# Query product of token tile 0 ahead of the first scores, x by ScalarE's queue and W by SyncE's

## The chip, the core and the metric

The kernel runs on one core of a Trainium2 chip. A core has TensorE (PE, matrix products; its weight loads are listed apart as PEld), VectorE (DVE), ScalarE (ACT), GpSimd (POOL) and SyncE (SP), each with its own instruction queue, worked off in order, and 16 DMA engines that all queues share. Times are device microseconds (us) of one execution. The metric is that time; the kernel before takes 636.64 us (median of three runs, 636.23 to 636.75).

## The reference

Three layers over 8 x 64 = 512 tokens of width 512, all in 32-bit floats. The change concerns the first one, a cross attention over a context of 1601 rows for each of the 8 sequences:

```python
def _L0_xattn_ref(proj_p, proj_q, W, b):     # proj_p = layernorm(x), proj_q = context
    trans_q = jnp.einsum('bqh,oh->bqo', proj_q, W) + b
    att_weights = jnp.einsum('bph,bqh->bpq', proj_p, trans_q)
    att_norm = jax.nn.softmax(att_weights, axis=-1)
    att_vec = jnp.einsum('bpq,bqh->bph', att_norm, proj_q)
    return jax.nn.relu(jnp.einsum('bph,oh->bpo', att_vec, W) + b)
x = x + _L0_xattn_ref(_layernorm(x), ctx_1024, W, b)
```

After it come a causal linear attention with a GELU network (2048 wide), and a mixture of 8 experts of which each token takes two. They fill the time from about 170 us to the end and are not changed.

## The kernel before, in words

The 512 tokens are four tiles of 128 tokens (t = 0 to 3); a tile holds two sequences (h = 0, 1) of 64 tokens. The kernel does not multiply the 1601 context rows by W. It multiplies the normalised tokens by W once ("query product", `pw_t`, 128 x 4 x 512) and takes scores between that and the transposed context.

The front, before the first scores:

- x comes in two halves (line 101), tiles 0 and 1 by SP's queue and tiles 2 and 3 by ACT's; then W by SP (line 113); then SP issues the stream of context tiles.
- 12 idle matmuls on PE (line 224) run while x is under way.
- `statistics` (lines 353 to 360: mean and variance on DVE, square root on ACT) and `normalize` (362 to 366, DVE) for tiles 0 and 1, then for 2 and 3. Their outputs `pn` live in the buffer `xin`.
- `turn_p(t)` (370 to 374): four transposes of a normalised tile on PE into a PSUM bank, copied by ACT into `p_t`, which lives in `h_t`.
- W is transposed whole, 16 transposes into four PSUM banks (line 405), which DVE copies to `w_t` (line 411). `w_t` is used for the output of the layer, from 70 us on.
- `pw_half(half, hc)` (379 to 390): the query product of two token tiles (256 columns) for one of four blocks of W; four products add up in a bank, and ACT copies the bank to `pw_t`. All four blocks of the first half come before the first scores; the four blocks of the second half stand one each behind the four score groups of tile 0 (line 607).

The attention loop. `key_group(t, g)` (441 to 464): the scores of tile t against a quarter g of the keys (401 or 398 columns), two sequences side by side in the array; ACT copies them out with a bias `pb`, which DVE computes from the normalised tiles and the vector b (417 to 423). After the fourth quarter `softmax(t)` runs: maximum on DVE (469), exponential on ACT (471). `turn_scores(t)` transposes the result on PE (485), `weigh(t, g)` (502 to 535) multiplies it by a group of 512 context rows; the last group adds the tail rows, and the very last context row, which DVE spreads with a shuffle (509). `turn_av` and `attended` (547) apply W, `add_and_normalize` and `turn_h` prepare the next layer's input, `values(t, n)` (575 to 587) computes its value product from `h_t` and the weights `wv`.

The order of the work on each engine is that of the program's text. Only SP's loads run ahead. `stream` (126) writes them into a list, `issue_to` (184) issues them in that order as far as places allow. Context tiles, `wv`'s second half and later weights share a ring of 12 places of 8 KB a partition; a place is free when its reader is `done`. DMAs of all queues take eight semaphores in turn, so SP issues a load when the one eight before it has landed. The list begins with the keys (0, 0), then b (`xb`), keys (0, 1) to (0, 3), the four last rows (`("last", t)`, 8 KB each, placed in parts of `v_sb`), the columns `col` (32 KB), then keys (1, 0) and (1, 1), and for each t in turn rows (t, 0), keys (t+1, 2), rows (t, 1), keys (t+1, 3), rows (t, 2), the tail, and keys (t+2, 0) and (t+2, 1).

Of the kernel before, what the change touches and what calls it, by code (L numbers as in the profile page):

```python
# [20 lines left out]
P = 128  # L21
# [27 lines left out]
def perceiver_kernel(  # L49
# [34 lines left out]
    def mm_bank(name):  # L84
        return ps.tile([P, 512], F32, tag="mm", name=name)
# [11 lines left out]


    xs = resid.tile([P, NT, D], F32, name="xs")
    for t, queue in ((0, nc.sync), (2, nc.scalar)):  # L100
        queue.dma_start(xs[:, t : t + 2, :], x[:, t : t + 2, :])
    moe = ctx.enter_context(tc.tile_pool(name="moe", bufs=1))
    mid = ctx.enter_context(ExitStack())
    xinp = mid.enter_context(tc.tile_pool(name="xinp", bufs=1))
# [21 lines left out]
    def stream(key, src):  # L126
        order.append((key, src))

    def stream_keys(t, g):
        if t < NT:  # L130
            for h in range(2):
                src = context_t[2 * t + h, D * SW * g : D * (SW * g + WIDTHS[g])]
                stream(("ctxT", t, g, h), src.rearrange("(p c k) -> p c k", p=P, c=KC))
# [7 lines left out]
    stream("xb", xb.partition_broadcast(4))  # L141
    for g in range(1, 4):
        stream_keys(0, g)
    for t in range(NT):
        stream(("last", t), context_last[t])
    stream("col", columns)
    for g in range(2):
        stream_keys(1, g)
    for t in range(NT):
        stream_rows(t, 0)  # L150
        stream_keys(t + 1, 2)
        stream_rows(t, 1)
        stream_keys(t + 1, 3)
        stream_rows(t, 2)
        stream(("tail", t), context_tail[t])
        for g in range(2):
            stream_keys(t + 2, g)
        if t == 0:
            stream(("wv", 0), wv[0])
        if t == NT - 2:  # L160
            stream(("wv", 1), wv[1])
# [214 lines left out]

    pw_t = xa.tile([P, KC, B * S], F32, name="pw_t")

    def pw_half(half, hc):
        cols = slice(half * 2 * P, (half + 1) * 2 * P)  # L380
        bank = mm_bank(f"pw_{half}_{hc}")
        for oc in range(KC):
            nc.tensor.matmul(
                bank[:, : 2 * P],
                w_sb[:, oc, hc * P : (hc + 1) * P],
                p_t[:, oc, cols],
                start=(oc == 0),
                stop=(oc == KC - 1),
            )
        nc.scalar.copy(pw_t[:, hc, cols], bank[:, : 2 * P])  # L390

    issue_to(len(order))

    for t in range(0, NT, 2):
        of = [statistics(xs[:, t + h, :], f"p_{t + h}") for h in range(2)]
        for h in range(2):
            normalize(pn[:, t + h, :], xs[:, t + h, :], *of[h], f"p_{t + h}")
        if t == 0:
            turn_p(0)
            turn_p(1)  # L400

            w_banks = [acc_bank(f"w_t_{hc}") for hc in range(KC)]
            for hc in range(KC):
                for oc in range(KC):
                    nc.tensor.transpose(
                        w_banks[hc][:, oc * P : (oc + 1) * P], w_sb[:, oc, hc * P : (hc + 1) * P], ident
                    )
    pw_half(0, 0)
    pw_half(0, 1)
    for hc in range(KC):  # L410
        nc.vector.tensor_copy(w_t[:, hc, :], w_banks[hc])
    turn_p(2)
    turn_p(3)
    pw_half(0, 2)
    pw_half(0, 3)

    nc.vector.stream_shuffle(xb_bc, xb_in, [0] * 32)
    pb = xa.tile([P, NT], F32, name="pb")
# [83 lines left out]
    def weigh(t, g):  # L502

        if g == 0:
            all_av[t] = acc_bank(f"av_{t}")
        av, e_t = all_av[t], all_et[t]
        if g == NG - 1:
            last_bc = xa2.tile([P, D], F32, tag="tmp", name=f"last_bc_{t}")
            nc.vector.stream_shuffle(last_bc, last_in[t], [0] * 32)
        rows = [need("ctx", t, g, h) for h in range(2)]  # L510
        for j in range(4):
            for h in range(2):
                nc.tensor.matmul(  # L513
                    av[h * S : (h + 1) * S, :],
                    e_t[:, 4 * g + j, h * S : (h + 1) * S],
                    rows[h][:, j, :],
                    start=(g == 0 and j == 0),
                    stop=False,
                )
        done(*[("ctx", t, g, h) for h in range(2)])  # L520
        if g == NG - 1:
            for h in range(2):
                nc.tensor.matmul(
                    av[h * S : (h + 1) * S, :],
                    e_t[h * S : (h + 1) * S, 4 * NG, :S],
                    need("tail", t)[h * S : (h + 1) * S, :],
                    start=False,
                    stop=True,
                )
            av_sb = all_av[t] = xa2.tile([P, D], F32, tag="tmp", name=f"av_sb_{t}")  # L530

            nc.vector.scalar_tensor_tensor(
                av_sb, last_bc, all_scores[t][:, LK - 1 : LK], av, ALU.mult, ALU.add
            )
            nc.vector.tensor_scalar(av_sb, av_sb, all_rinv[t], None, ALU.mult)
# [66 lines left out]
            ALU.add,  # L602
        )

    for g in range(4):
        key_group(0, g)
        pw_half(1, g)
    for g in range(2):
        key_group(1, g)
    for t in range(NT):  # L610
# [10 lines left out]
        weigh(t, 1)  # L621
        if t == NT - 1:
            turn_h(t - 1)
        key_group(t + 1, 3)
        if 0 < t < NT - 1:
            values(t - 1, 0)
        weigh(t, 2)
        if t == NT - 2:
            late_loads()
# [1129 lines left out]
```

## Time and profile before

| what | value |
|---|---|
| median of three runs | 636.64 us (636.23 to 636.75) |
| profiled execution | 636.05 us, span 634.3 us |
| PE busy | 617.5 us, 97% of the span |
| DVE, ACT, POOL busy | 182.8, 120.0, 64.1 us |
| mean granted clock of PE | 0.994 |
| DMA | 131.74 MB, mean 208 GB/s, 406 to 428 GB/s from 10 to 160 us |
| first transposes of x on PE | 8.42 us from the span's start |
| first scores of tile 0 | 20.66 us |
| first scores of tile 1 | 39.74 us |

A line of the time line reads: start, duration (both us), engine, line of the kernel, operation, output<-inputs, shape, count; in brackets the idle time before it and what ended that. Equal neighbours are merged, and a duration runs from the first start to the last end. A 32-bit product is two rows (passes) in the trace, a transpose one. A line of the table of stretches gives the stretch, its length, each engine's busy time with its number of instructions, the granted clock of PE (1.00 is full), the DMA engines' busy share and the GB/s moved. A line of the list of waits reads: who waited <- for whom: us in total, times, longest. A queue row reads: queue, packets, MB, share of the DMA engines' time; queue q1 is SP's, q10 ACT's, q0 POOL's.

### The profile page before, as it was taken

What the parts mean: (1) busy time and instruction counts of PE and PEld (TensorE: products, weight loads), DVE (VectorE), ACT (ScalarE), POOL (GpSimd) and SP (SyncE); (2) the same over time, 40 slices, a digit from 0 to 9 for tenths busy, and PEclk for the clock granted to TensorE, in tenths of its full rate; (3) what the DMA queues carried; (4) which work ended last, traced back from release to release, by engine and by line L of the source; (5) the groups of instructions that cost most, each with busy time, mean ns of one, the idle gap of its engine ahead of it and who ended that gap; (6) DMA issues with size and microseconds to landing.
All of it is one profiled execution on the core that took longest, in us unless ns stands there. A gap on an engine that the chain in (4) does not pass through costs nothing. (4 is left out here: it accounts for less than half of the span.)

```text
span 634.3 us, 8728 instructions
## 1 busy us (share of the span) xinstructions
PE 617.5 (97%) x3572; PEld 352.2 (56%) x3572; DVE 182.8 (29%) x433; ACT 120.0 (19%) x225; POOL 64.1 (10%) x87
## 2 busy tenths in 40 slices
PE   7999999999999999999999999999999999999994
PEld 7653434343444444455444447966783667775793
DVE  5111322333326888670000026501311101011100
ACT  2241332320132122031111111301101101111110
POOL 4000000000000000050000002241210121301100
PEclk8999999999999999999999999999999999999998
DMA  8999999999421203030312121426890477784711
GB/s 352 409 422 425 423 422 423 425 428 421 199 67 57 77 2 134 0 132 1 122 35 109 67 100 67 168 79 240 300 367 3 165 295 272 298 327 143 296 19 17
DMA packets 23617, 131.74 MB, mean 208 GB/s; under 512 B 4068, under 2 KB 4068, under 8 KB 12168
## 3 DMA queue, kind: packets, MB, share of 16 engines
q1 hardware_dynamic: 19064, 121.80, 48.5%
q0 software_dynamic: 3248, 7.58, 4.8%
q10 hardware_dynamic: 1248, 1.59, 0.8%
q8 instruction: 38, 0.62, 0.4%
q14 instruction: 19, 0.16, 0.1%
HBM read 126.05 MB, written 4.91 MB: 206 GB/s over the span
## 5 line engine op out<-in xcount | busy, mean ns | idle before, releaser
L1261 PEld LDWEIGHTS up<-xgT,e_up 128*128 128x128 f32 x896 | 100.7, 192 | 4.5 <-ACT y_sb L1239 2.5
L1261 PE MATMUL up<-xgT,e_up 128*128 128x128 f32 x896 | 101.6, 275 | 1.0 <-PEq L1589 0.6
L1227 DVE TENSOR_TENSOR mid<-up,act 128x256 f32<-128x256 f32 x38 | 16.1, 425 | 149.2 <-ACT act L1225 149.2
L1275 PE MATMUL y<-e_wo,mid 128*128 128x512 f32 (+1 forms) x144 | 58.8, 547 | 0.0
L858 PE MATMUL hid<-v_sb,w 128*128 128x512 f32 (+2 forms) x144 | 56.6, 545 | 0.0
L879 PE MATMUL mlp<-w,hid_sb 128*128 128x512 f32 x112 | 51.0, 597 | 0.0
L452 PE MATMUL sc<-ctxT,pw_t 128*64 128x401 f32 (+1 forms) x256 | 46.1, 503 | 0.0
L513 PE MATMUL av<-ctx,eT 128*64 128x512 f32 x192 | 43.5, 597 | 0.0
L858 PEld LDWEIGHTS hid<-v_sb,w 128*128 128x128 f32 x144 | 26.2, 190 | 29.1 <-issue 27.3
L1225 ACT ACTIVATE act<-up 128x256 f32<-128x256 f32 x38 | 14.6, 384 | 120.5 <-PE up L1261 96.7
L1275 PEld LDWEIGHTS y<-e_wo,mid 128*128 128x128 f32 x144 | 25.7, 190 | 20.5 <-issue 17.8
L1240 POOL DMA_INDIRECT out_dram<-y_sb,dst_late x12 | 18.3, 1528 | 166.8 <-ACT y_sb L1239 96.8
L879 PEld LDWEIGHTS mlp<-w,hid_sb 128*128 128x128 f32 x112 | 20.7, 190 | 23.5 <-issue 23.4
L873 POOL TENSOR_TENSOR xin<-xin,b_bc 128x512 f32<-128x512 f32 x4 | 5.1, 1268 | 268.4 <-DVE rstd_h L815 265.0
L452 PEld LDWEIGHTS sc<-ctxT,pw_t 128*64 128x64 f32 x256 | 17.5, 136 | 26.0 <-issue 25.8
L666 PE MATMUL wk<-h_t,wk 128*128 128x512 f32 x64 | 29.5, 604 | 0.0
L666 PE MATMUL wq<-h_t,wq 128*128 128x512 f32 x64 | 29.4, 602 | 0.0
L583 PE MATMUL v<-wv,h_t 128*128 128x512 f32 x64 | 29.2, 599 | 0.0
L777 PE MATMUL wo<-wo,a_t 128*128 128x512 f32 x64 | 28.9, 599 | 0.0
L927 DVE TENSOR_TENSOR xs<-mlp,xs 128x512 f32<-128x512 f32 x3 | 2.1, 691 | 86.5 <-PE mlp L879 86.5
L751 DVE RECIPROCAL rden<-rden 128x512 f32<-128x512 f32 x8 | 26.8, 3353 | 0.3
L513 PEld LDWEIGHTS av<-ctx,eT 128*64 128x64 f32 x192 | 13.0, 136 | 24.2 <-issue 23.9
(263 smaller groups left out, 627.8 us busy)
## 6 DMA issues: line engine op xcount, KB each, us to landing
e_up<-in_L_ffn_up_dram SPq DMA_DIRECT2D x32, 1024.0 KB, 5.3
ctx<-in_ctx_dram SPq DMA_DIRECT2D x24, 1024.0 KB, 17.3
ctxT<-in_ctx_T_dram SPq DMA_DIRECT2D x24, 802.0 KB, 13.3
e_wo<-in_L_ffn_wo_dram SPq DMA_DIRECT2D x16, 1024.0 KB, 10.3
w<-in_L_attn_w_dram SPq DMA_DIRECT2D x8, 1024.0 KB, 6.9
ctxT<-in_ctx_T_dram SPq DMA_DIRECT2D x8, 796.0 KB, 16.2
wv<-in_L_attn_wv_dram SPq DMA_DIRECT2D x2, 1024.0 KB
wq<-in_L_attn_wq_dram SPq DMA_DIRECT2D x2, 1024.0 KB, 17.8
```

The source lines that it names most:

```text
L452: nc.tensor.matmul(sc[h * S : (h + 1) * S, :width], pw_t[:, c, (2 * t + h) * S : (2 * t + h + 1) * S], keys[h][:, c, :], start=(c == 0), s ...
L513: nc.tensor.matmul(av[h * S : (h + 1) * S, :], e_t[:, 4 * g + j, h * S : (h + 1) * S], rows[h][:, j, :], start=(g == 0 and j == 0), stop=F ...
L583: nc.tensor.matmul(bank, h_t[:, c, t * P : (t + 1) * P], wv_n[:, c, :], start=(c == 0), stop=(c == KC - 1))
L666: nc.tensor.matmul(bank, w[:, c, (j % 4) * P : (j % 4 + 1) * P], h_t[:, c, :], start=(c == 0), stop=(c == KC - 1),)
L751: nc.vector.reciprocal(rden, rden)
L777: nc.tensor.matmul(wo_banks[t], a_t[:, j, t * P : (t + 1) * P], wo_r[j // 4][:, j % 4, :], start=(j == 0), stop=(j == nj - 1),)
L858: nc.tensor.matmul(hid_banks[f][:, tokens], w[:, c, (f % 4) * P : (f % 4 + 1) * P], h2_t[:, c, tokens], start=(c == 0), stop=(c == KC - 1),)
L879: nc.tensor.matmul(acc[t], hid[:, t * P : (t + 1) * P], need("w2", f // 4)[:, f % 4, :], start=(f == 0), stop=(f == FF // P - 1),)
L1227: nc.vector.tensor_tensor(hid, bank[:, FQ:], act, ALU.mult)
L1240: nc.gpsimd.indirect_dma_start(out=out, out_offset=bass.IndirectOffsetOnAxis(ap=dst[:n, :], axis=0), in_=y_sb[:n, :], in_offset=None, boun ...
L1261: nc.tensor.matmul(bank[:, m * P : (m + 1) * P], up_of[q][:, c, m * P : (m + 1) * P], xg_t[c], start=(c == 0), stop=(c == KC - 1),)
L1275: nc.tensor.matmul(bank[:, :width], h_t[:, j * P : (j + 1) * P], w[:, 2 * (q % 2) + j, n * width : (n + 1) * width], start=(q + j == 0), s ...
```

## The change

x is split into tile 0 and tiles 1 to 3, both issued by ACT; W becomes SP's first load. Tile 0 alone is normalised, transposed and multiplied ahead of the first scores; half of W (two blocks) is transposed there, copied by ACT. Tiles 1 to 3 are normalised on DVE meanwhile, transposed behind the first score group, and multiplied in one row of four products of 384 columns behind the second; the other half of W is transposed behind that and copied by DVE. The last rows and the columns leave their place behind the keys of tile 0: `("last", t)` goes just ahead of rows (t, 2), `col` ahead of `wv`. In the loop, `values(t - 1, 0)` changes places with `key_group(t + 1, 3)`, and `weigh` asks for its rows before the shuffle.

```diff
     xs = resid.tile([P, NT, D], F32, name="xs")
-    for t, queue in ((0, nc.sync), (2, nc.scalar)):
-        queue.dma_start(xs[:, t : t + 2, :], x[:, t : t + 2, :])
+    nc.scalar.dma_start(xs[:, :1, :], x[:, :1, :])
+    nc.scalar.dma_start(xs[:, 1:, :], x[:, 1:, :])
...
         stream_keys(0, g)
-    for t in range(NT):
-        stream(("last", t), context_last[t])
-    stream("col", columns)
     for g in range(2):
         stream_keys(1, g)
...
         stream_keys(t + 1, 3)
+        stream(("last", t), context_last[t])
         stream_rows(t, 2)
...
         if t == 0:
+            stream("col", columns)
             stream(("wv", 0), wv[0])
...
-    def pw_half(half, hc):
-        cols = slice(half * 2 * P, (half + 1) * 2 * P)
-        bank = mm_bank(f"pw_{half}_{hc}")
+    def query(hc, first, n):
+        cols = slice(first * P, (first + n) * P)
+        bank = mm_bank(f"pw_{first}_{hc}")
         for oc in range(KC):
             nc.tensor.matmul(
-                bank[:, : 2 * P],
+                bank[:, : n * P],
                 w_sb[:, oc, hc * P : (hc + 1) * P],
                 p_t[:, oc, cols],
                 start=(oc == 0),
                 stop=(oc == KC - 1),
             )
-        nc.scalar.copy(pw_t[:, hc, cols], bank[:, : 2 * P])
+        nc.scalar.copy(pw_t[:, hc, cols], bank[:, : n * P])
+
+    def turn_w(hc, copy):
+        bank = acc_bank(f"w_t_{hc}")
+        for oc in range(KC):
+            nc.tensor.transpose(bank[:, oc * P : (oc + 1) * P], w_sb[:, oc, hc * P : (hc + 1) * P], ident)
+        copy(w_t[:, hc, :], bank)
...
-    for t in range(0, NT, 2):
-        of = [statistics(xs[:, t + h, :], f"p_{t + h}") for h in range(2)]
-        for h in range(2):
-            normalize(pn[:, t + h, :], xs[:, t + h, :], *of[h], f"p_{t + h}")
-        if t == 0:
-            turn_p(0)
-            turn_p(1)
-
-            w_banks = [acc_bank(f"w_t_{hc}") for hc in range(KC)]
-            for hc in range(KC):
-                for oc in range(KC):
-                    nc.tensor.transpose(
-                        w_banks[hc][:, oc * P : (oc + 1) * P], w_sb[:, oc, hc * P : (hc + 1) * P], ident
-                    )
-    pw_half(0, 0)
-    pw_half(0, 1)
-    for hc in range(KC):
-        nc.vector.tensor_copy(w_t[:, hc, :], w_banks[hc])
-    turn_p(2)
-    turn_p(3)
-    pw_half(0, 2)
-    pw_half(0, 3)
+    normalize(pn[:, 0, :], xs[:, 0, :], *statistics(xs[:, 0, :], "p_0"), "p_0")
+    turn_p(0)
+    for hc in range(2):
+        turn_w(hc, nc.scalar.copy)
+    for some in ((1, 2), (3,)):
+        of = [statistics(xs[:, t, :], f"p_{t}") for t in some]
+        for t, (mv, std) in zip(some, of):
+            normalize(pn[:, t, :], xs[:, t, :], mv, std, f"p_{t}")
+        for hc in range(3) if len(some) == 2 else (3,):
+            query(hc, 0, 1)
...
+        rows = [need("ctx", t, g, h) for h in range(2)]
         if g == NG - 1:
             last_bc = xa2.tile([P, D], F32, tag="tmp", name=f"last_bc_{t}")
             nc.vector.stream_shuffle(last_bc, last_in[t], [0] * 32)
-        rows = [need("ctx", t, g, h) for h in range(2)]
...
-    for g in range(4):
+    key_group(0, 0)
+    for t in range(1, NT):
+        turn_p(t)
+    key_group(0, 1)
+    for hc in range(KC):
+        query(hc, 1, NT - 1)
+    for hc in range(2, KC):
+        turn_w(hc, nc.vector.tensor_copy)
+    for g in range(2, 4):
         key_group(0, g)
-        pw_half(1, g)
...
-        key_group(t + 1, 3)
         if 0 < t < NT - 1:
             values(t - 1, 0)
+        key_group(t + 1, 3)
```

## The prediction

> **What bounds the kernel now.** I read the page first, then the time line of TensorE (PE) over the first 46 us, the list of waits, the table of stretches with the clock, and last the transfers of the streaming stage. The page says which engine holds the end:
>
> ```profile
> span 634.3 us, 8728 instructions
> PE 617.5 (97%) x3572; PEld 352.2 (56%) x3572; DVE 182.8 (29%) x433; ACT 120.0 (19%) x225; POOL 64.1 (10%) x87
> ...
> PEclk8999999999999999999999999999999999999998
> DMA  8999999999421203030312121426890477784711
> ```
>
> PE is busy from slice 2 to the last but one; the DMA engines are full too, but only in the first ten slices (to 159 us). So a microsecond taken out of PE's queue early is kept to the end, as long as the loads of those ten slices keep up. The span is 634.3 us, the profiled execution 636.05 us (1.75 us lie outside the span), the median of the runs 636.64 us, 0.59 above it.
>
> The time line of PE to the first scores of token tile 1:
>
> ```profile
> 8.42 1.77 PE L373 MATMUL tr_p<-ident,xin 128*128 128x128 f32 x8 [2.20 <-DVE xin L366]
> 9.98 2.97 PE L405 MATMUL w_t<-ident,w_sb 128*128 128x128 f32 x16
> 12.78 3.62 PE L383 MATMUL pw<-h_t,w_sb 128*128 128x256 f32 x16
> 16.24 1.04 PE L373 MATMUL tr_p<-ident,xin 128*128 128x128 f32 x8
> 17.11 3.62 PE L383 MATMUL pw<-h_t,w_sb 128*128 128x256 f32 x16
> 20.66 2.92 PE L452 MATMUL sc<-ctxT,pw_t 128*64 128x401 f32 x16
> 23.51 1.99 PE L383 MATMUL pw<-h_t,w_sb 128*128 128x256 f32 x8
> ...
> 39.74 5.62 PE L452 MATMUL sc<-ctxT,pw_t 128*64 128x401 f32 x32
> 45.29 1.53 PE L485 MATMUL et<-ident,scores 128*128 128x128 f32 x12
> ```
>
> The one idle stretch is the 2.20 us before 8.42, and the list of waits tells its chain: x, then VectorE (DVE).
>
> ```profile
> DVE st_p L355 <- DMA xs<-in_x_dram: 6.0, 1, 6.0
> ...
> PE tr_p L373 <- DVE xin L366: 2.2, 1, 2.2
> ```
>
> That gap has a second price, in the clock (columns: stretch, then busy time of each engine, then the granted clock):
>
> ```profile
> 5.31:8.72 3.41, 1.21 (x11) 1.02 (x11) 2.55 (x8) 0.59 (x2) 2.41 (x13) 1.00 1.02 427
> 8.72:12.13 3.41, 3.41 (x19) 3.23 (x18) 2.86 (x9) 1.55 (x4) 0.00 (x0) 0.50 1.02 424
> ...
> 623.12:626.53 3.41, 2.36 (x11) 1.73 (x10) 0.48 (x1) 0.47 (x1) 0.00 (x0) 1.00 0.00 0
> ```
>
> After 3.41 us in which PE was busy for 1.21 (36%) the clock is halved for the next 3.41 us; after a stretch with 2.36 busy (69%) it is not. The threshold lies between. In the halved stretch a 128-column pass takes 0.213 us, otherwise 0.109 (eight transposes from 16.24 to 17.11), so it costs 16 passes, about 1.7 us.
>
> **The change, part by part.** The reference point is the start of the first scores of tile 1, now 39.74; everything after it is the same work in nearly the same order. S is the start of the first scores of tile 0, now 20.66.
>
> *PE's work after S.* Scores 2.85 (20.66 to 23.51); 12 transposes at 0.109 plus 0.25 for the changes of shape, 1.56; scores 2.85; 32 passes of 384 columns at 1.5 x 0.216 (16 passes from 12.78 to 16.24), 10.4; 8 W transposes, 1.07; two score groups at 2.78 (39.74 to 45.29), 5.55. Sum 24.3, so the gain is 39.74 - 24.3 - S = 15.45 - S. The product itself is not cheaper: 32 x 0.112 for tile 0 (the idle matmuls of 128 columns start 0.112 apart at full clock) plus 32 x 0.324 is 13.95 us against 64 x 0.216 = 13.8.
>
> *When PE starts.* DVE needs only tile 0. From the landing of x it was 0.7 + 0.2 + ScalarE's (ACT) 0.3, then 0.35 lost because DVE was at tile 1, then reciprocal and normalise: 2.4 us. Without tile 1 it is 2.05. When does tile 0 land? Its 128 rows of 2 KB go by ACT's queue while W's 128 rows of 8 KB go by SyncE's (SP). Two busy queues get one row each in turn, whatever its size: in the stretch 560 to 561, with 8 KB rows on one and 2 KB rows on the other, the queue rows are
>
> ```profile
> q1 hardware_dynamic: 37, 0.29, 72.7%
> q0 software_dynamic: 34, 0.06, 33.2%
> ```
>
> So tile 0 is not four times as fast. About a quarter of its rows pass before SP's queue starts (of the first 24 packets, to 3.0 us, 16 were ACT's); 96 pairs of 10 KB at the 0.41 MB/us of 3 to 5 us take 2.4, and landing was told some 0.35 after the last row: about 5.7. Bounds: 4.8 (shares by bytes) and 6.2 (all of W first), against 5.8 and 6.0 now. PE then starts at 5.7 + 2.05 = 7.75, 0.65 earlier. W (7.2 us from issue to landing before) has its last rows beside ACT's 6 KB rows and lands at about 6.6; even with the old 7.2 it is there at 8.0, before the first W transpose.
>
> *The clock.* Idle matmuls to 6.2 and work from 7.75 make 0.9 + 0.97 of the 3.41 us to 8.72: 55%, between the known 36% and 69%, slightly nearer the upper end in distance. I take full clock. Then tile 0's transposes end at 8.25, eight W transposes at 9.1, ACT's copy of tile 0 (0.59) at 9.1; 32 passes at 0.112 and a change of shape give S = 12.9, gain 2.55. With the halved clock: 16 passes by 12.13, the remaining 20 take 2.2, S = 14.5, gain 0.95.
>
> The Trainium skill (TensorE: Matmul & The Clock Gate, Part 4) says that transposes do not count as busy for this gate. By that rule the new stretch holds only the idle matmuls' 0.9 us, 27%, the clock is halved, and the sum is the 0.95. The stretch 8.72 to 12.13 holds transposes alone (lines 373 and 405) and the clock rises at its end, so here the trace contradicts the rule.
>
> *What else S waits for.* Keys of group 0: x, W and two key tiles are 3.74 MB; 3.1 MB had moved by 10 us, the rest at 0.418 MB/us is there at 11.5, told by 12.4 at the latest (SP's next issue, held by that landing, comes at 12.46). Margin 0.5. On ACT, two W copies (0.59 each, moved from DVE) and the roots of tiles 1 and 2 now stand before the copies of the product, the root of tile 3 before the last one. Tiles 1 to 3 have 6 KB rows in turn with keys of 6.4 KB: 8 rows an engine at 0.5 us a pair from 5.3, landing about 9.7. Statistics of two tiles (0.87 each), root, two normalisations (0.65 each), statistics and root of tile 3 end at 14.0, its copy at 14.3; the scores need it three quarters in, at S + 2.05 = 15.0. Margin 0.7.
>
> *The softmax of tile 0.* A quarter of the second-half product (1.93 us) stood behind the last scores; without it 5.55 us of scores cover copy, maximum, exponential: 0.59, 1.82, 1.63 and handovers, 4.35. Hidden by 1.2.
>
> *The stream.* The four last-row loads and the columns leave the place behind the keys of tile 0. There SP held them in flight instead of big tiles, and at 22 to 25 us the DMA engines moved 365 GB/s instead of 423: 0.4 us of supply comes back (none if each small load costs as much in its new place, 1.1 if the whole gap between landings closes). PE's earlier clock needs it. The tightest load that the new order leaves where it was is the second row group of tile 1: issued, time to landing, used:
>
> ```profile
> 62.34 0.33 SPq L201 DMA_DIRECT2D ctx<-in_ctx_dram  x1
> ...
> DMA to landing us min/median/max: 18.1/18.1/18.1
> ...
> 82.20 3.65 PE L513 MATMUL av<-ctx,eT 128*64 128x512 f32 x16
> ```
>
> 80.4 against 82.2: 1.8 us. The gain can't exceed 1.8 + 0.4 = 2.2 (1.8 to 2.9) from there on. The next key group (used at 85.69) was tighter, but is moved behind 3.65 us of value product, which has had its weights since about 67; the softmax that loses that cover keeps over 13 us. SP's queue passes one small load at a time, and none is needed before its own row group. The shuffle behind the row request costs nothing: same DVE queue, PE ends 4.7 us later.
>
> *Sum.* Gain min(2.55, 2.2) = 2.2 us, 0.3 of it lost again at 80 us: 636.05 - 2.2 = 633.85 for the profiled execution, 634.4 at the median.
>
> The Trainium skill (DMA: Bandwidth & Descriptors, Queues, rings and completion order) lets a DMA engine drain a packet of some 9 to 17 descriptors before it changes queue. By that, tile 0 (8 rows an engine) would pass in one go and PE would hardly stop after the idle matmuls; S would be bound by the keys at 12.4, and the row group at 82 would still hold the gain to 2.2. The 37 to 34 packets above speak for single rows.
>
> **Rivals.** (1) *The clock is halved all the same* (threshold above 55%, or another place of the 3.41 us): gain 0.95, 635.7. For it, halving at 36%; against, a gap of 1.5 us instead of 2.2. (2) *It does not bring what its first line says*: tile 0 lands at 6.2 because W's long rows go in turn with it; PE starts at 8.25, 43% busy, halved, S = 15.0, gain 0.45: 636.2. The row-by-row sharing speaks for it, the head start against. (3) *Slower: ACT's queue holds the product.* Tiles 1 to 3 by ACT's queue arrive late, the roots hold the copies, PE stops in the first scores and the transposes. Each microsecond past 10.4 costs one: nothing is left at 12.6, and beyond 13.9 it is slower by over 0.2%; landing at 14.5 gives 638.3. For it, x now lands at 6.0 whole and this part shares with the keys; against, equal turns. (4) *The stream binds*: small loads cost 0.2 each in their new places and the supply ends 0.5 to 1 later, gain about 1: 635.6.
>
> **How the numbers follow.** The measurement tells 0.2%, 1.27 us (635.37 to 637.91), from no change. Forecast 0.52 (own range 633.7 to 635.3), clock halved 0.22, tile 0 no sooner 0.10, ACT's queue 0.08, stream 0.08. Faster: 0.50 of the forecast and 0.07 of (1) and (4) make 0.57; slower: 0.08 of (3) and 0.06 for what I don't see, 0.14; same 0.29. The range runs from a gain of 3.0 (tile 0 at 4.8 and supply 1.1 earlier) to (2): 633.6 to 636.4.
>
> **What would show it.** Right: the first transposes near 7.75, no 0.50 clock after 8.72, first scores near 12.9, tile 1's near 37.2, a wait of PE on the row load near 80. Wrong: a halved clock, PE waiting on ACT's copy or for tiles 1 to 3 between 13 and 17 us, or on keys before 20 us.

## The result, and the profile after

The changed kernel takes 637.33 us (median of 17 runs, 636.50 to 638.37); the kernel before, run beside it, 636.23 us (17 runs, 635.43 to 637.27). The ratio is 1.0017, with a 95% interval from 1.0009 to 1.0024. The change costs 1.1 us, where 2.2 were to be won; 637.33 lies outside the forecast's range of 633.6 to 636.4. The profiled execution of the changed kernel took 637.39 us, 1.34 more than that of before.

The page of the changed kernel, the lines that answer to those of before:

```profile
span 635.7 us, 8725 instructions
PE 617.5 (97%) x3572; PEld 351.4 (55%) x3572; DVE 181.8 (29%) x431; ACT 121.0 (19%) x227; POOL 64.1 (10%) x87
...
PEclk8999999999999999999999999999999999999998
DMA  8999999999411203030312121527890477784711
```

PE does the same amount of work in as many instructions; the span is 1.4 us longer because PE stands still for longer. The time line of PE shows where:

```profile
9.67 0.66 PE L372 MATMUL tr_p<-ident,xin 128*128 128x128 f32 x4 [2.74 <-DVE xin L365]
10.16 1.45 PE L394 MATMUL w_t<-ident,w_sb 128*128 128x128 f32 x8
11.40 5.00 PE L382 MATMUL pw<-h_t,w_sb 128*128 128x128 f32 x32
16.34 2.92 PE L445 MATMUL sc<-ctxT,pw_t 128*64 128x401 f32 x16
19.19 1.53 PE L372 MATMUL tr_p<-ident,xin 128*128 128x128 f32 x12
20.64 2.92 PE L445 MATMUL sc<-ctxT,pw_t 128*64 128x401 f32 x16
23.50 10.59 PE L382 MATMUL pw<-h_t,w_sb 128*128 128x384 f32 x32
...
34.89 11.00 PE L445 MATMUL sc<-ctxT,pw_t 128*64 128x401 f32 x64
45.81 1.53 PE L478 MATMUL et<-ident,scores 128*128 128x128 f32 x12
```

The new order is there: four transposes, half of W, tile 0's product, scores. But it starts at 9.67 us, where before began at 8.42 and the forecast put 7.75, and the idle time ahead of it has grown from 2.20 to 2.74 us. The product of tile 0, 32 passes that take 3.74 us at full clock (in e1 below), takes 5.00. At 45.81 the kernel is 0.52 us behind before (45.29).

The time line of DVE in the same stretch:

```profile
7.59 0.69 DVE L354 BATCH_NORM_STATS2 st_p<-xs 128x6 f32<-128x512 f32 x1 [7.59 <-DMA xs<-in_x_dram]
...
9.07 0.55 DVE L365 TENSOR_SCALAR xin<-xs,mv_p,rstd_p 128x512 f32<-128x512 f32 x1
11.41 0.69 DVE L354 BATCH_NORM_STATS2 st_p<-xs 128x6 f32<-128x512 f32 x1 [1.80 <-DMA xs<-in_x_dram]
```

Tile 0, a quarter of x, is there at 7.59 us. Before, half of x was there at 6.03. Tiles 1 to 3 follow at 11.4. The table of stretches (length, busy time of PE, PEld, DVE, ACT and POOL with instruction counts, PE's granted clock, DMA share, GB/s) has the second half of the loss:

```profile
7.23:10.64 3.41, 0.97 (x9) 0.97 (x10) 1.59 (x4) 0.57 (x2) 0.71 (x3) 1.00 1.01 417
10.64:14.06 3.42, 3.42 (x19) 3.42 (x17) 2.51 (x8) 2.12 (x6) 0.00 (x0) 0.50 1.02 426
```

PE was busy for 28% of a stretch, and the clock was halved for the next 3.42 us. The profiled execution loses another 0.9 us in two places of the expert layer, at 424 and 571 us, which the change does not touch. The kernels below lose or gain up to 0.8 us there in their profiled executions, so I don't put this part down to the change. The front thus accounts for some 0.5 us of the 1.1 between the medians; no run shows where the rest arises.

### The profile page after: what moved, and what is told of

Same layout as the page of the kernel before. It is cut to its first block, busy times and chain, and to the rows that moved or that the text cites. A ratio compares the mean times of both kernels' runs of the same rounds, so it can differ in the third digit from the quotient of the medians.

```text
span 635.7 us, 8725 instructions
## 1 busy us (share of the span) xinstructions
PE 617.5 (97%) x3572; PEld 351.4 (55%) x3572; DVE 181.8 (29%) x431; ACT 121.0 (19%) x227; POOL 64.1 (10%) x87
```

## The experiments

Each time is a median, each ratio is taken to the kernel before, run beside it on the same chip (636.41 us for the first four kernels, 635.97 for the next four, 636.14 and 636.13 for the last two groups). The theory after the result: x by one queue beside W by the other makes tile 0 late, this alone costs the 1.9 us of PE's start and, through the longer gap, the clock; the rest of the change does what the forecast says. The rivals: the other loads or the new order cost in themselves; or the queues are right and something after 17 us is wrong.

| kernel | us | ratio, 95% interval | PE's first transposes at | softmax transposes of tile 0 at |
|---|---|---|---|---|
| before, profiled | 636.05 | | 8.42 | 45.29 |
| changed | 637.33 | 1.0017 [1.0009, 1.0024] | 9.67 | 45.81 |
| e1, x in halves | 634.59 | 0.9977 [0.9968, 0.9985] | 7.81 | 42.44 |
| e2, one queue | 635.27 | 0.9983 [0.9974, 0.9991] | 6.78 | 42.55 |
| e3, small loads back | 637.42 | 1.0017 [1.0008, 1.0026] | 9.51 | 45.65 |
| e4, queues alone | 641.43 | 1.0080 [1.0067, 1.0093] | 12.99 | 50.83 |
| e5, before with 21 idle products | 640.48 | 1.0066 [1.0052, 1.0080] | 8.52 | 43.73 |
| e6, changed with 26 | 635.63 | 0.9992 [0.9983, 1.0001] | 10.28 | 44.80 |
| e8, e1 with the small loads back | 635.59 | 0.9998 [0.9989, 1.0007] | 8.27 | 44.44 |
| e10, e1 with `wv` later | 633.79 | 0.9968 [0.9956, 0.9980] | 8.28 | 42.86 |
| e14, tile 0 ahead of W | 634.59 | 0.9978 [0.9969, 0.9988] | 7.80 | 42.38 |
| e12, e10 with W split | 636.71 | 1.0012 [1.0002, 1.0021] | 9.55 | 46.01 |
| e11, e10 with 18 idle products | 636.32 | 1.0006 [0.9996, 1.0015] | 7.64 | 42.25 |
| e13, before with 18 | 638.51 | 1.0042 [1.0024, 1.0060] | 8.45 | 43.85 |
| e15, queues exchanged | 635.90 | 0.9993 [0.9983, 1.0002] | 9.46 | 46.67 |
| e16, e10 with tile 0 on both | 634.71 | 0.9980 [0.9970, 0.9990] | 7.19 | 43.27 |

### The queues: undone, done alone, on one queue

e1 is the changed kernel with x loaded as before:

```diff
-    nc.scalar.dma_start(xs[:, :1, :], x[:, :1, :])
-    nc.scalar.dma_start(xs[:, 1:, :], x[:, 1:, :])
+    for t, queue in ((0, nc.sync), (2, nc.scalar)):
+        queue.dma_start(xs[:, t : t + 2, :], x[:, t : t + 2, :])
```

> The changed kernel, but x in halves again: tiles 0 and 1 by SyncE's queue ahead of W, tiles 2 and 3 by ScalarE's. Theory 1 (the loss is tile 0's landing: its 2 KB rows go in turn with W's 8 KB rows, 7.5 us instead of 6.0): tile 0 is there at 6.0, the first transposes start near 8.1 instead of 9.67, the first scores near 14.8 instead of 16.3, and the time is 1.3 to 1.8 us under the changed kernel's, 635.5 to 636.0, below the kernel before. Theory 2 (the new order of the work itself, ScalarE's copies and roots or the loads in the loop, costs the time): the front is earlier, but the time stays at 637.0 to 637.5.

634.59 us. The time line of PE (two pieces of it):

```profile
7.81 0.65 PE L372 MATMUL tr_p<-ident,xin 128*128 128x128 f32 x4 [1.78 <-DVE xin L365]
9.29 3.74 PE L382 MATMUL pw<-h_t,w_sb 128*128 128x128 f32 x32
12.96 2.92 PE L445 MATMUL sc<-ctxT,pw_t 128*64 128x401 f32 x16
...
79.35 4.60 PE L506 MATMUL av<-ctx,eT 128*64 128x512 f32 x16
83.88 3.70 PE L576 MATMUL v<-wv,h_t 128*128 128x512 f32 x8
```

This is the forecast's course: first transposes at 7.81 (7.75 was forecast), first scores at 12.96 (12.9), tile 0's softmax transposes 2.85 us ahead of before (2.55). Then the 16 passes at 79.35, which take 3.65 us in every kernel where their rows are there, take 4.60. The list of waits has the cause:

```profile
PEld av L506 <- DMA ctx<-in_ctx_dram: 0.8, 1, 0.8
```

The row group lands at 80.26 us, 0.9 us after PE has come to it, and from there on 1.85 us of gain are left, 1.9 at the end of the span: the 2.2 less 0.3 that the forecast allowed. So everything that the forecast said behind the first landing holds, and the two lines that load x are the loss.

e4 does these lines alone, in the kernel before:

```diff
-    for t, queue in ((0, nc.sync), (2, nc.scalar)):
-        queue.dma_start(xs[:, t : t + 2, :], x[:, t : t + 2, :])
+    nc.scalar.dma_start(xs[:, :1, :], x[:, :1, :])
+    nc.scalar.dma_start(xs[:, 1:, :], x[:, 1:, :])
```

> The kernel before, with the new queues alone: x by ScalarE's queue, tile 0 apart from tiles 1 to 3, and W by SyncE's. VectorE normalises tile 0 only behind the statistics of tile 1. Theory 1: tile 1 lands near 11.4, the first transposes start near 13.0 instead of 8.42, and all of it stays: 4.3 to 5.2 us over the kernel before, about 641. Theory 2 (the landing isn't what counts): within 1 us of the kernel before.

641.43 us, 0.8% slower. DVE's time line, then PE's:

```profile
7.55 0.69 DVE L355 BATCH_NORM_STATS2 st_p<-xs 128x6 f32<-128x512 f32 x1 [7.55 <-DMA xs<-in_x_dram]
...
11.40 0.69 DVE L355 BATCH_NORM_STATS2 st_p<-xs 128x6 f32<-128x512 f32 x1 [2.93 <-DMA xs<-in_x_dram]
```

```profile
12.99 1.97 PE L373 MATMUL tr_p<-ident,xin 128*128 128x128 f32 x8 [7.00 <-DVE xin L366]
```

The landings are those of the changed kernel (7.59 and 11.41). The old order needs tiles 0 and 1 before it starts, so it waits for the second. The queues cost 5 us in the old order, which also has the clock halved from 8.24 to 18.48 us; in the new order, which needs tile 0 alone, they cost 2.5 (the changed kernel against e1).

e2 puts all of x on SP's queue: tile 0, W, tiles 1 to 3, then the keys.

```diff
-    nc.scalar.dma_start(xs[:, :1, :], x[:, :1, :])
-    nc.scalar.dma_start(xs[:, 1:, :], x[:, 1:, :])
+    nc.sync.dma_start(xs[:, :1, :], x[:, :1, :])
     nc.sync.dma_start(w_sb, xw)
+    nc.sync.dma_start(xs[:, 1:, :], x[:, 1:, :])
```

> The changed kernel, but all of x by SyncE's queue: tile 0, then W, then tiles 1 to 3, then the keys. Theory 1: tile 0 has the DMA engines to itself, lands near 4.2, and the first transposes follow the idle matmuls at 6.3 to 6.9; W is there at about 6.5, tiles 1 to 3 at about 8.1; the first scores are bound by the keys at about 12.4, 3.9 us earlier than in the changed kernel. At 80 us the loads hold it: the time is 2 to 3.5 us under the changed kernel's, 633.8 to 635.3. Theory 2: no more than 0.5 us under the changed kernel's.

635.27 us. Tile 0 has nothing beside it and PE starts at 6.78, but between 3 and 4 us the DMA engines move 150 GB/s (418 in e1), and all that follows is late by the difference. PE's time line:

```profile
11.88 0.89 PE L445 MATMUL sc<-ctxT,pw_t 128*64 128x401 f32 x2
13.08 2.91 PE L445 MATMUL sc<-ctxT,pw_t 128*64 128x401 f32 x14 [0.31 <-DMA ctxT<-in_ctx_T_dram]
...
81.16 3.65 PE L506 MATMUL av<-ctx,eT 128*64 128x512 f32 x14 [0.37 <-DMA ctx<-in_ctx_dram]
```

PE waits for the keys, so that a start 1.0 us ahead of e1 is worth nothing at 42 us, and then for rows that land 0.85 us later than in e1.

### What takes tile 0 so long

e14 changes one line of the changed kernel: tile 0 goes by SP's queue ahead of W.

```diff
-    nc.scalar.dma_start(xs[:, :1, :], x[:, :1, :])
+    nc.sync.dma_start(xs[:, :1, :], x[:, :1, :])
```

> The changed kernel with tile 0 of x taken from ScalarE's queue and put on SyncE's, ahead of W; tiles 1 to 3 stay on ScalarE's. Theory (tile 0 is late because its 128 rows of 2 KB go in turn, one for one, with W's rows of 8 KB): beside rows of 2 KB tile 0 has 0.5 MB to wait for instead of 1.25 MB, lands by about 4.8 us instead of 7.5, and PE's first transposes start at about 6.9 instead of 9.67; W lands no sooner (about 7.3), so its transposes start there and the query product at about 8.3 (11.40 in the changed kernel). Then the stream of keys and rows stops PE at its second row group of tile 1, as in the kernel with x in halves: 634.6 us, 0.997. Rival (the second queue is slow by itself, or 128 rows take their time whatever stands beside them): tile 0 lands at 6 or later, the query product starts no sooner than 9.5, 635.5 or more.

The time is the expected one, 634.59, with the same wait for the row group. But tile 0 lands at 5.7, not 4.8:

```profile
5.72 0.69 DVE L354 BATCH_NORM_STATS2 st_p<-xs 128x6 f32<-128x512 f32 x1 [5.72 <-DMA xs<-in_x_dram]
```

The expectation had a wrong row size in it. The rows of tiles 1 to 3 are read as one row of 6 KB, not as three of 2; 128 pairs of 2 + 6 KB are 1.0 MB, as much as e1's 128 pairs of 4 + 4, and e1's tile lands at 5.68. Taking turns row by row explains both. It does not explain the changed kernel: 128 pairs of 2 + 8 KB are 1.25 MB, 0.25 more, which is 0.6 us, not 1.8.

e12 starts from e10 (below) and has tile 0 beside half rows of W:

```diff
-    for t, queue in ((0, nc.sync), (2, nc.scalar)):
-        queue.dma_start(xs[:, t : t + 2, :], x[:, t : t + 2, :])
+    nc.sync.dma_start(xs[:, :1, :], x[:, :1, :])
...
-    nc.sync.dma_start(w_sb, xw)
+    nc.scalar.dma_start(w_sb[:, :2, :], xw[:, :2, :])
+    nc.scalar.dma_start(xs[:, 1:, :], x[:, 1:, :])
+    nc.sync.dma_start(w_sb[:, 2:, :], xw[:, 2:, :])
```

> The kernel with x in halves and the value weights' load put back, with its first loads in another order: tile 0 of x alone on SyncE's queue and behind it one half of W; on ScalarE's the other half of W and behind it tiles 1 to 3. By turns of one row each, tile 0 (2 KB rows) goes beside 4 KB rows of W: 0.75 MB, landed by about 5.3 us; the rest of W goes beside rows of tile 1: another 0.75 MB, by about 7.2. PE starts at about 7.4 (7.81 to 8.28 with x in halves) and needs W at 7.9. The rows of tile 1 had some 2 us to spare, so nothing downstream takes it back: 633.4 us, 0.996. Rival (the keys bind: all that is ahead of them is as much as before, they land at 12.3, and PE needs them 5.15 us after its start): no more than 0.1 us is won over the kernel with the value weights late, 633.8.

A clear miss: 636.71 us, 2.9 above e10.

```profile
7.48 0.69 DVE L356 BATCH_NORM_STATS2 st_p<-xs 128x6 f32<-128x512 f32 x1 [7.48 <-DMA xs<-in_x_dram]
```

With only 0.75 MB to wait for, tile 0 is as late as in the changed kernel. So the bytes beside it are not the matter. What the DMA engines moved in each microsecond, from the view of the transfers (GB/s):

| kernel, what stands at the heads of the queues | 2–3 us | 3–4 | 4–5 | 5–6 | DVE begins tile 0 at |
|---|---|---|---|---|---|
| before, x and x | 115 | 397 | 414 | 451 | 6.03 |
| e1, x and x | 131 | 418 | 422 | 463 | 5.68 |
| e14, x and x | 180 | 395 | 453 | 463 | 5.72 |
| changed, x and W | 106 | 317 | 414 | 338 | 7.59 |
| e12, x and half of W | 145 | 170 | 248 | 244 | 7.48 |
| e2, x alone, then W | 201 | 150 | 428 | 410 | 4.63 |
| e4, x and W | 66 | 401 | 397 | 336 | 7.55 |
| e15, W and x (below) | 106 | 324 | 410 | 317 | 7.39 |

Wherever W's rows begin in the first microseconds the rate falls somewhere before 6 us. The mean rate is not all: e4, with the first loads of the changed kernel, moves 401 GB/s from 3 to 4 us and has tile 0 as late. There the 16 DMA engines end their shares of tile 0 1.2 us apart (5.85 to 7.01 us). In the trace's packets the first 13 rows of W in the changed kernel took 1.07 us each and the next six 0.91, against 0.31 for most later ones; in before, where W's rows begin at 4.9 us, the first nine took 0.31. The first rows of x are slow too (0.84 us each for 16 rows of 4 KB in before), but of the next 24 half took their normal 0.16, and only one more than 0.35.

Two further kernels test whether this is W or the queue. e15 exchanges the two queues of the changed kernel:

```diff
-    nc.scalar.dma_start(xs[:, :1, :], x[:, :1, :])
-    nc.scalar.dma_start(xs[:, 1:, :], x[:, 1:, :])
+    nc.sync.dma_start(xs[:, :1, :], x[:, :1, :])
+    nc.sync.dma_start(xs[:, 1:, :], x[:, 1:, :])
...
-    nc.sync.dma_start(w_sb, xw)
+    nc.scalar.dma_start(w_sb, xw)
```

> The changed kernel with its two first loads exchanged: all of x on SyncE's queue, W at the head of ScalarE's. Theory (any load that starts with rows of W at once is slow in its first microseconds, and drags what takes turns with it): tile 0 lands at 7 us or later, PE starts at 9.2 or later, 637.3. Rival (SyncE's queue is served ahead of ScalarE's, so that tile 0 on it is in sooner): it lands by 6.2, PE starts by 8.3 with the clock left full, and the time is that of the kernel with x in halves, 634.6.

Tile 0 lands at 7.39 and PE starts at 9.46: it is W at the head, not the queue. The total, 635.90, is 1.4 below the expectation. The profiled execution was the slowest of its ten (637.6, with two halved stretches on end; the ten run from 634.6 to 637.6), so its trace does not show where the median execution gains over the changed kernel; that stays open.

e16 is e10 with tile 0 split by rows over both queues, nothing beside it:

```diff
-    for t, queue in ((0, nc.sync), (2, nc.scalar)):
-        queue.dma_start(xs[:, t : t + 2, :], x[:, t : t + 2, :])
+    nc.sync.dma_start(xs[:64, :1, :], x[:64, :1, :])
+    nc.scalar.dma_start(xs[64:, :1, :], x[64:, :1, :])
+    nc.scalar.dma_start(xs[:, 1:, :], x[:, 1:, :])
```

> The kernel with x in halves and the value weights' load put back, with tile 0 of x split by rows over both queues ahead of everything, W behind it on SyncE's, tiles 1 to 3 on ScalarE's. Theory (rows of W at the head are what is slow): tile 0 (0.25 MB, nothing beside it) lands by about 4.5 us, and W, in turn with rows of 6 KB, at about 7.9; PE's first transposes start at about 6.7, those of W at 7.9, the query product at about 8.8 (9.64 in the kernel that it is made from), and 0.5 to 0.8 us come through: 633.2 us, 0.996. Rival (W behind a short load of x is slow all the same, its rows being cold): W lands at 8.5 or later, the query product starts no sooner than 9.4, and the time is 633.8 or more.

Tile 0 lands at 5.1, W at 8.2: 0.3 to 0.6 later than the theory had them, W before the rival's 8.5. W's first six rows took 0.67 us each, and 148 GB/s were moved from 3 to 4 us, so W is slow behind a short load too. The query product starts at 9.11 (8.8 expected), and then a wait that neither had foreseen takes more than that back, in PE's time line:

```profile
13.72 2.99 PE L447 MATMUL sc<-ctxT,pw_t 128*64 128x401 f32 x16 [0.87 <-ACT pw_t L391]
```

ACT's copies of the product, ready to be made from 10 us on, stand behind the roots of tiles 1 and 2, whose x lands at 11.4; the second root ends at 13.5. That is the forecast's third rival, at a price of 0.87 us; here the product is ready sooner than tiles 1 to 3 are. At 43.27 the kernel is 0.41 us behind e10, and near 98 us it loses another 0.7 to keys that e10 doesn't wait for. 634.71 us, 0.9 above e10, though the intervals of the two ratios overlap.

### The clock

e6 and e5 make the gap ahead of the first transposes too short to halve the clock: more idle products in the changed kernel (26 for 12) and in the kernel before (21 for 12).

```diff
-NIDLE = 12
+NIDLE = 26
```

> The changed kernel with 26 idle matmuls in place of 12, which keep PE busy up to about 9.2 to 10.0, where tile 0's transposes start anyway (9.67). If the halved clock behind the gap is a cost of its own, no 0.50 shows, tile 0's front (8 W transposes and 32 passes) runs at full pace, and the time falls by 1.2 to 2.2 us, to 635.1 to 636.1. If only the landing counts, it stays at 637.3, or rises by as much as the idle matmuls run over.

635.63 us. The table of stretches has full clock right through:

```profile
7.61:11.02 3.41, 3.41 (x32) 3.41 (x32) 1.52 (x4) 0.40 (x2) 0.33 (x1) 1.00 1.03 426
```

From the first transposes to the softmax transposes PE needs 34.52 us (10.28 to 44.80), in the changed kernel 36.14: the halved clock costs 1.62 us, the 1.7 of the forecast. The added products push PE's start back by 0.61, so 1.01 us of it show at 45 us. The clock is thus a part of the changed kernel's loss of its own, on top of the late tile. The time falls by 1.6 us (1.0017 to 0.9992), more than that; a place where more is won is seen below.

> The kernel before with 21 idle matmuls in place of 12, to about 8.1 to 8.9. If the halving costs 1.7 us there too, the front comes 1.2 to 1.7 us earlier; the key group of tile 2 used at 85.69 had landed 1.35 us before its use, so at most about 1.4 stays: 634.8 to 635.4. If the halving does not matter: 636.2 to 636.6.

640.48 us, 5 us off the expectation, and the largest surprise of the study. The front is 1.55 us shorter, as expected. The stream takes 1.25 of it back by 92 us (without the change the row group lands at 81.50, later than in e1). The rest comes at 425 and 549 us:

```profile
423.96 1.88 PE L1313 MATMUL up<-e_up,xgT 128*32 128x512 f32 x10 [0.61 <-ACTq L1587]
427.30 2.77 PE L1313 MATMUL up<-e_up,xgT 128*32 128x512 f32 x22 [1.46 <-issue]
...
548.65 0.43 PE L1215 MATMUL xgt<-ident,xg 32*128 32x32 f32 x4
551.35 0.60 PE L1215 MATMUL xgt<-ident,xg 128*128 128x128 f32 x4 [2.28 <-issue]
```

PE stops in the middle of a group and nothing that the profile shows releases it ("issue"). The second hole leaves PE busy for 33% of its stretch, and the clock is halved behind it:

```profile
548.99:552.40 3.41, 1.13 (x8) 0.94 (x7) 0.34 (x1) 0.27 (x1) 0.00 (x0) 1.00 0.02 5
552.40:555.81 3.41, 3.41 (x5) 1.36 (x5) 0.35 (x1) 0.00 (x0) 0.00 (x0) 0.50 0.89 303
```

In the second hole, from 548.9 to 551.4 us, the view of the transfers has one packet in all, on the queue of instructions:

```profile
DMA packets 1, 0.02 MB, mean 7 GB/s; under 512 B 0, under 2 KB 0, under 8 KB 0
...
q8 instruction: 1, 0.02, 2.2%
```

It ends at 549.99, and PE goes on 1.36 us later; at 425 a packet of the same queue ends at 426.01 and PE goes on 1.29 us later. In the stops of before, e11, e13 and e14 shown as "issue" near 425 and 549 us such a packet ends 1.28 to 1.52 us before PE goes on.

e13 repeats it in the kernel before with 18 idle products, e11 with 18 in e10.

> The kernel before with 18 idle products instead of 12 (21 gave 640.48: its front was 1.55 us shorter, the stream took 1.25 of it back at 80 us, and then PE stood still for 2.3 us in the middle of a group of transposes at 549 us and for 1.5 us at 425 us, each until 1.3 us after a packet on the queue that fetches its code, and the clock was halved behind the first). Theory (these holes come of how the code falls into packets, which each number of products shifts): with 18 they are elsewhere or nowhere; if nowhere, 635.7. Rival (idle products before the first transposes cost in themselves): about 640 again, with the same holes.

638.51 us, between the two. The holes are there, a little further on in the code:

```profile
425.01 1.92 PE L1313 MATMUL up<-e_up,xgT 128*32 128x512 f32 x16 [0.56 <-ACTq L1587]
428.55 1.92 PE L1313 MATMUL up<-e_up,xgT 128*32 128x512 f32 x16 [1.62 <-issue]
```

And the kernel before has the same hole, almost hidden:

```profile
424.40 3.63 PE L1313 MATMUL up<-e_up,xgT 128*32 128x512 f32 x28 [0.57 <-ACTq L1587]
428.22 1.05 PE L1313 MATMUL up<-e_up,xgT 128*32 128x512 f32 x4 [0.19 <-issue]
```

Each product is two passes. With 24 passes at the start the stop comes after 28 passes of this group, with 36 after 16, with 42 after 10. It moves by exactly the number of passes added, so it stands at a fixed count of PE's instructions. By the same count the 52 passes of e6 put it at the head of the group, where PE waits for ACT's queue anyway; there the 32 passes take 3.64 us. From the group's start to the next group it is 4.80 us with 24 passes in before (4.73 in the changed kernel), 5.39 with 36, 6.05 with 42, and 3.58 in e6. So both kernels lose 1.2 us here themselves, which is more than enough for the rest of e6's gain. That the place of the stop is set by the number of instructions ahead is shown. That PE waits there for code is read from the packet that ends 1.3 to 1.5 us ahead each time; what makes the packet come late is not shown.

> The kernel with x in halves and the value weights' load put back, with 18 idle products at the start instead of 12, so that PE has no gap before its first transposes in which the clock could be halved. Theory (the halved clock is drawn anew in each execution, by where its 3.41-us windows fall, and PE's gap of 1.3 to 1.8 us is too short for it in nearly all): no change, 633.8. Rival (half of the executions are caught): 633.0. Third (the added products move PE's code against the packets in which it is fetched, and PE stands still somewhere later): a hole of 2 us or more in the trace that no load and no engine explains, 636 or more.

636.32 us, 2.5 above e10: the third of the three cases, except that there are two holes of 1.2 us and not one of 2. The front came out best of all (softmax transposes at 42.25, 3.0 us ahead of before). Two holes (idle of 1.19 and 1.18 us before lines 1314 and 1276, at 425 and 549) and a wait of 0.5 for keys near 97 are in the trace, and at the end of the span 0.4 is left. That execution is the fastest of its ten, so the trace doesn't hold all that the median lost. Both kernels with 18 and the one with 21 are slower than the same kernel with 12, although the front of each is earlier.

### The small loads and the value weights

e3 is the changed kernel with the last rows and the columns back behind the keys of tile 0; e8 is the same in e1. Both have this edit:

```diff
     for g in range(1, 4):
         stream_keys(0, g)
+    for t in range(NT):
+        stream(("last", t), context_last[t])
+    stream("col", columns)
...
-        stream(("last", t), context_last[t])
         stream_rows(t, 2)
...
-            stream("col", columns)
             stream(("wv", 0), wv[0])
```

> The changed kernel, but the last rows and the columns at their old place behind the keys of tile 0. Theory 1: PE never waits for the stream in either, so the time is that of the changed kernel, 637.33 within 0.4. Theory 2 (the small loads inside the loop cost): 0.5 to 1.1 us under the changed kernel's.

637.42 us, the changed kernel's time. The row group lands at 81.48 instead of 81.23, and nothing waits for it.

> x in halves as in the first experiment (634.59), and the last rows and the columns back at their old place. In the first experiment PE was 2.85 us ahead of the kernel before until 79 us and then waited for context rows, and 1.85 stayed. If the small loads at their new place are what brings those rows earlier, the rows land up to 0.4 us later without that and the time is 634.8 to 635.1; if their place does not matter, it is 634.6 within 0.3.

635.59 us, 1.0 above e1 (1.3 by the ratios). Two things differ in the profiled execution: the clock was halved (36% busy from 5.07 to 8.48), and the row group lands at 81.30 instead of 80.26. In these two pairs the row group lands 0.25 and 1.04 us later with the small loads at their old place (0.4 was forecast, 0 to 1.1). In this execution PE comes to the rows at 81.36, when they are there, so that here the halved clock alone is the loss; at full clock, with e1's 79.35, it would have had to wait for the landing at 81.30. How much of the 1.0 us between the medians is this and how much the clock, these runs do not tell.

e10 is e1 with the first half of the value weights streamed behind the row group for which e1 waits:

```diff
         stream_rows(t, 1)
+        if t == 1:
+            stream(("wv", 0), wv[0])
...
-            stream(("wv", 0), wv[0])
```

> x in halves as in the first experiment, and the value weights (1 MB, used near 83 us) loaded behind the second row group of tile 1 instead of ahead of tile 1's rows. If that row group's landing (80.26 us against a use at 79.35) is what took 1.0 us of the front's gain back, it now lands near 77.9, the wait at 79 us is gone, and the time is 0.6 to 1.0 us under the first experiment's, 633.6 to 634.0. If the gain is lost to something else: 634.6 within 0.3.

633.79 us, 0.9968: the fastest here, and faster than both kernels. Its interval overlaps that of e1, so the times alone do not show the 0.6 to 0.8 us between the two; the trace shows the wait. The rows land at 77.8 and the wait is gone, as PE's time line shows; the weights land at 80.27 and are used at 83.36. The front of its profiled execution began 0.47 us later than e1's, so that 0.5 us of the 0.9 are left at 83 us (83.36 against 83.88):

```profile
79.77 3.65 PE L507 MATMUL av<-ctx,eT 128*64 128x512 f32 x16
83.36 3.70 PE L577 MATMUL v<-wv,h_t 128*128 128x512 f32 x8
```

## Why the prediction was wrong

The step that failed is "When PE starts", and in it the sentence "About a quarter of its rows pass before SP's queue starts". There was no head start. From 2 to 3 us ACT's queue (q10) moved 4 rows and SP's (q1) 12:

```profile
q1 hardware_dynamic: 12, 0.10, 67.0%
q10 hardware_dynamic: 4, 0.01, 2.1%
```

The forecast had read its head start from one execution of before, in the same stretch:

```profile
q10 hardware_dynamic: 20, 0.08, 47.3%
q1 hardware_dynamic: 8, 0.03, 8.0%
```

There ACT's first row came at 1.85 us and SP's at 2.75. In e1 and e11, with the same two loads, SP's came first (at 1.85, ACT's at 2.78 and 2.26), so which queue is first differs between executions; this one reading was taken for a rule. From 2 to 8 us the two queues of the changed kernel went row for row, as the forecast's own row had said:

```profile
q1 hardware_dynamic: 194, 1.36, 63.4%
q10 hardware_dynamic: 195, 0.58, 25.7%
```

The rate of 0.41 MB/us, taken from before for the time from 3 us on, held in one microsecond of three (317, 414, 338 GB/s, after 106 from 2 to 3), since W's rows at the head of a queue are slow. And a landing is that of the slowest of 16 DMA engines: their end packets for W and tile 0 are spread over 1.1 us, from 5.97 to 7.06, where in e1 those for x come within 0.7. The last row of tile 0 ended at 7.05 us, where the forecast has 5.35, and DVE began 0.5 us after it, for which the forecast has 0.35. By these four rates 1.18 MB had moved by 6 us, so by bytes alone the 1.25 MB of W and tile 0 would be in by 6.2, the forecast's upper bound; DVE got tile 0 at 7.59. The value rested on a head start that was not there, and the bound on a mean rate that says nothing of the slowest engine.

Point by point:

- *Tile 0 lands*: 5.7 forecast (4.8 to 6.2), 7.5 measured. W: 6.6 forecast, 7.4 measured. Tiles 1 to 3: 9.7 forecast, 11.4 measured.
- *From landing to PE*: 2.05 forecast; 9.67 - 7.59 = 2.08 measured. Right.
- *Clock*: full was forecast for a gap of 1.5 us. With e1's gap of 1.78 PE is 48% busy and the clock stays full, so the choice was right for the gap assumed, but with some luck: where the 3.41 us begin differs between executions, and e8, with the same first loads as e1, had a gap of 2.17 us, 36% and half clock. With 2.74 us and 28% it was halved. From PE's start to the first scores 6.67 us instead of 5.15. With 1.92 for the start this makes S = 16.34, not 12.9: 3.44 us, which is the whole failure.
- *PE's work after S*: 24.3 forecast, 23.98 measured (16.34 to 40.32). Right.
- *ACT's queue, keys, softmax*: no wait in the changed kernel. The margin on ACT was used up only in e16.
- *The stream*: the row group named in the forecast is where e1, e2 and e14 wait; 2.2 less 0.3 forecast, 1.85 left in e1. Right.
- *Small loads*: 0.4 forecast, 0.25 and 1.04 measured in the two pairs.
- *Sum*: S = 16.34 and the tail of 23.98 put the first scores of tile 1 at 40.32, 0.58 later than before. The rest of the profiled execution's 1.34 comes after 400 us, in the places named above. Two small sums of the forecast are off without a part in this: a landing at 14.5 in rival (3) makes 638.5, not 638.3, and the start at 8.25 in rival (2) leaves PE 41% busy, not 43%.

Of the rivals the second, "tile 0 lands at 6.2 because W's long rows go in turn with it", named the mechanism that decided, together with the first; its price was 1.3 us too low, because 6.2 was a bound by mean rate. It should have been carried on to the point where it turns into a loss: with 6.67 us from PE's start, S passes 15.45 when tile 0 lands after 6.7 us, only 0.5 past that bound.

The Trainium skill (DMA: Bandwidth & Descriptors, Queues, rings and completion order) has an engine drain a packet of some 9 to 17 descriptors from one queue before it turns to the next, so that the 8 rows of tile 0 on an engine would have passed in one go. The 194 and 195 rows in this stretch are against that as well; the measurement decides.

On the clock the Trainium skill (TensorE: Matmul & The Clock Gate, Part 4) says that transposes do not bring the full clock, since they do not count as busy in the same way. Two stretches here speak against it. In e4 one with 1.17 us of idle products and nothing else was followed by half clock. In e1 one that began with 1.12 us of idle products (4.92 to 6.04) and ended with 0.53 us of transposes, from 7.81, was followed by full clock:

```profile
4.82:8.24 3.42, 1.17 (x10) 0.97 (x9) 0.69 (x1) 0.00 (x0) 2.84 (x15) 1.00 0.94 356
```

```profile
4.92:8.34 3.42, 1.64 (x14) 1.34 (x13) 2.22 (x5) 0.29 (x1) 3.00 (x14) 1.00 1.04 435
```

## What to carry to other kernels

Estimate when a first load lands from the slowest DMA engine and from the first rows' own durations, not from the mean rate of a stretch in full flow, and take a bound from the pairing of loads that the change makes. What must be there first should stand at the heads of both queues, and the large weight behind it: here x on both queues ahead of W was worth 0.4%, 2.5 us, over x beside W. And a gain in the front is worth what the next wall lets through: find the load that will be late then (here a row group at 80 us), and move ahead of it nothing that has time.

## What the runs showed of the hardware that had not been expected

- Where W's rows began before 4 us, the first 6 to 14 of them took 0.65 to 1.1 us each on average (kernels changed, e2, e15 and e16, and e12 with half rows); where they began at 4.9 us or later, 0.31 (before, e1 and e14). Why is open.
- The clock goes by stretches of 3.41 us whose place differs between executions (the first one at full clock began anywhere from 4.8 to 7.6 us), so the same gap can be caught in one and not in another. Busy shares of 28 to 36% were followed by half clock; 44% (at the end of e11), 46, 48 and 61% were not. At half clock, 61% (e4) and 65% (e15) were not enough to bring it back; a stretch without gaps was.
- PE can stand still for 1 to 2.3 us at a fixed count of its instructions, until some 1.4 us after a packet on the queue of instructions. Twelve more passes at the start of the kernel showed as holes at 427 and 551 us.
